# Node stages in quads, edge attributes by the pair, and the second MLP product as four 64x64 quadrants

## The chip, the core and the metric

The kernel runs on one core of a Trainium2 chip. The metric is the device time of one execution in microseconds (us); lower is better. Its engines are TensorE (PE; loading its weights is PEld), VectorE (DVE), ScalarE (ACT), GpSimd (POOL) and the DMA engines; SP issues most of the DMAs.

## The reference

One graph attention layer in fp32 with a residual, for 12,500 nodes of 128 features and 400,000 edges sorted by destination:

```python
h = relu(layernorm(x))
msg_src = h @ w_src + b_src
msg_dst = h @ w_dst
rad = silu(silu(edge_attr_32 @ w1 + b1) @ w2 + b2) @ w3 + b3      # 32 -> 64 -> 64 -> 128
m = (msg_src[src] + msg_dst[dst]) * edge_weight * rad
a, v = per head of 8: (m @ w_sep + b_sep)                          # 16 + 16 columns a head
score = sum(leaky(a) * alpha_dot)
att = softmax of score over the edges of one destination
out = x + segment_sum(v * att, dst) @ w_proj + b_proj
```

## The kernel before

**Node stage.** The nodes are 98 blocks of 128 rows (the last has 84). They are loaded at once and taken in groups of 14 blocks. `stats` (L196 to L201, DVE and ACT) and `norm` (L209, ACT) make the normalised rows of group g + 1, then `products` turns and multiplies group g in quads of four blocks: transposes into PSUM (L220, PE), a copy to hT (L223, DVE), products with w_src and w_dst side by side (L230, PE), the source half copied out by ACT (L237), the destination half by DVE with b_src added (L238). Every group ends with two stores into the tables t_src and t_dst. After the second group `ends_and_cuts` compares the destinations and writes the ends of the sections. A branch on `bad` follows; then `windows` zeroes and loads the block-diagonal weights (w1b, w2b, w3b, b12), computes b_s, and reads the ends back (L606 to L641).

**Loop.** The edges are 400 pairs of two sections of 500. `step(k)` is called for k = -5 to 399 and 14 times more; its statement order is each engine's order, since scheduling is manual. It handles several pairs at once: loads on SP for k + 3; eight indirect gathers on POOL of t_src rows for pair k + 4 (L718, four buffers `gs`, each freed by the transposes of its pair); for pair k the third MLP product (L758), rad on DVE (L761), the transposes of the gathered rows and the destination part into pm (L770, L775), their product with rad, mT (L779); for pair c = k - 12 the value products (L864, L866) and the sums over destinations (L875), whose PSUM tile misc ACT copies to ob (L879) and SP stores; for pair k the attention product (L783, L785, L787); the first MLP product of pair k + 2 (L736, h1 on ACT L739), the second of k + 1 (L744, h2 on ACT L746); the turned attributes of k + 3 (L728 into bank m1, L730). Odd steps end with the scores (L794, also in misc), steps with k mod 8 = 3 turn the softmax (L838, also in misc).

The order of TensorE's work in a step is third product, L770, L775, values of section 0, attention of section 0, values of section 1, first product, second product, attention of section 1, sums, turned attributes, scores. The second product is one matmul of 128x128 weights (two 64x64 blocks on the diagonal, the rest zero) by 500 columns, and its bank m1 is also the one that the turned attributes use. The first and the third product use the two banks of p3. An fp32 matmul shows up as two instructions in the profile.

Attributes come in groups of eight pairs, by eight strided DMAs (L693), two in the first step of a group, one in each of the next six and none in the last.

**Final stage.** After the loop and a last scatter into agg (L1067), the nodes are taken in groups of 14: x + b_out on POOL (L1162), the quotients by the softmax sums on DVE (L1165 to L1168), then in quads the transposes (L1179, PE), qT (L1182, ACT), a correction added to x on DVE (L1185), the product with w_proj (L1186, PE), its sum with x (L1190, DVE), and one store for a group.

Of the kernel before, what the change touches and what calls it, by code (L numbers as in the profile page):

```python
# [30 lines left out]
P = 128  # L31
C = 128
# [21 lines left out]
EP = 8  # L54
# [3 lines left out]
def gnn_kernel(ctx: ExitStack, tc: tile.TileContext, a: dict, out: bass.AP):  # L58
# [18 lines left out]
    agg = dram.tile([N + W, ROW], F32, name="agg")  # L77
    win = dram.tile([NS * W, ROW], F32, name="win")
    base_d = dram.tile([2, NP], I32, name="base_d")
# [15 lines left out]
    x_v = x[0:NF * P, :].rearrange("(p t) c -> p t c", t=NF)  # L95
    ident = const.tile([P, P], F32, name="ident")
# [48 lines left out]
    with tc.tile_pool(name="node", bufs=2) as np_, tc.tile_pool(name="node1", bufs=1) as n1, \  # L145
# [6 lines left out]
        b_nodes = n1.tile([P, C], F32, name="b_nodes")  # L152
        nc.scalar.dma_start(out=b_nodes, in_=a["b_src"].to_broadcast([P, C]))
# [6 lines left out]
        last = n1.tile([1, 2, NP], I32, name="last")  # L160
# [3 lines left out]
        nc.sync.dma_start(out=prev[1:RP, :], in_=dst[RC - 1:E - 1].rearrange("(p c) -> p c", c=RC))  # L164
        with nc.allow_non_contiguous_dma(reason="the sections' ends"):
            for f in range(2):
                nc.sync.dma_start(out=base[:, f, :], in_=dst_h[f:f + 1, :, 0])
                nc.sync.dma_start(out=last[:, f, :], in_=dst_h[f:f + 1, :, SEC - 1])
# [16 lines left out]
        spans = groups[:-1] + [(groups[-1][0], NB)]  # L185
        hs = {}

        def rows(t):
            return P if t < NF else tail

        def stats(g):
            t0, t1 = spans[g]
# [11 lines left out]
        def norm(g):  # L204
            t0, t1 = spans[g]
            hs[g] = np_.tile([P, XG, C], F32, name="h")
            for t in range(t0, t1):
                n = rows(t)
                nc.scalar.activation(hs[g][:n, t - t0, :], x_all[:n, t, :], AF.Relu,  # L209
                                     bias=shift[:n, t:t + 1], scale=rstd[:n, t:t + 1])  # L210

        def products(g):
            t0, t1 = spans[g]
            ms = np_.tile([P, 2, XG, C], F32, name="ms")
            for u0 in range(t0, t1, 4):
                us = range(u0, min(u0 + 4, t1))
                pt = nps.tile([P, 4, P], F32, name="pt")
                for u in us:
                    n = rows(u)
                    nc.tensor.transpose(pt[:, u - u0, :n], hs[g][:n, u - t0, :], ident[:n, :n])  # L220
                hT = np_.tile([P, 4, P], F32, name="hT")
                w = (len(us) - 1) * P + rows(us[-1])
# [58 lines left out]
        for g in range(G):  # L281
# [4 lines left out]
            if g == 1:  # L286
                ends_and_cuts()
# [950 lines left out]
```

## Time and profile before

| | |
|---|---|
| median of 3 runs | 6550.76 us (6549.27 to 6562.26) |
| profiled execution, its own time | 6566.2 us |
| its span | 6564.2 us |
| mean TensorE clock granted | 0.873 |
| busy: PE, DVE, ACT, POOL | 77%, 44%, 27%, 47% |
| first gather, first L770 | 215.9 us, 240.5 us |
| last ob, first data of the final stage | 6393.9 us, 6424.7 us |
| DMA packets | 884,920, of them 527,255 under 512 B |

Busy time is that of the engine's instructions in the profiled execution; the end of a matmul is modelled. A row of the costliest groups gives line, engine, operation, out<-in, shapes and count, then busy us and mean ns of one, then the engine's idle time just before these instructions and what ended most of it. In a timeline row the bracket holds the idle time before the instruction and its releaser. A row of a stretch gives start:end, its length, busy us (and instructions) of PE, PEld, DVE, ACT and POOL, the granted clock as a share of full speed, the DMA engines' busy share and GB/s.

### The profile page before, as it was taken

How to read it: one execution, taken by the hardware profiler on the slowest of the kernel's cores; microseconds unless marked ns; L12 is line 12 of the kernel's file. 1: busy time of each engine (PE TensorE's matmuls, PEld its weight loads, DVE VectorE, ACT ScalarE, POOL GpSimd, SP SyncE). 2: the span in 40 equal slices, each digit the busy share in tenths (PEclk: the TensorE clock that was granted, in tenths of full speed). 3: DMA queues.
4: the chain of work that ended last, by engine and by line, in shares of the span. 5: the costliest groups of instructions: out<-in, count | busy, mean ns of one | idle time of the engine just before them, and what ended most of it. 6: DMA issues, size and time to landing. Idle time of an engine off the chain costs nothing. (4 is left out here: it accounts for less than half of the span.)

```text
span 6564.2 us, 79188 instructions
## 1 busy us (share of the span) xinstructions
PE 5066.2 (77%) x26490; PEld 2665.6 (41%) x26490; DVE 2887.1 (44%) x5210; ACT 1785.1 (27%) x3797; POOL 3111.5 (47%) x3231
## 2 busy tenths in 40 slices
PE   3477878787878878788788787887887878888774
PEld 2234444444444444444444444444444444444453
DVE  4234444444444444444444444444444444444465
ACT  3122222222222222222222222222222222222221
POOL 0455555455554545544455454454554545545402
PEclk7688898898998989988888898898888989888885
DMA  3454444444444444444444444444444444444423
GB/s 124 135 144 119 124 119 115 125 117 121 121 122 118 121 119 119 124 117 115 123 120 121 119 116 121 122 115 120 121 117 122 119 120 121 124 119 118 114 60 123
DMA packets 884920, 783.25 MB, mean 119 GB/s; under 512 B 527255, under 2 KB 773279, under 8 KB 884250
## 3 DMA queue, kind: packets, MB, share of 16 engines
q1 hardware_dynamic: 778482, 560.72, 31.0%
q0 software_dynamic: 102816, 210.37, 13.6%
q10 hardware_dynamic: 3202, 6.99, 0.3%
q8 instruction: 212, 3.47, 0.2%
q14 instruction: 208, 1.70, 0.1%
HBM read 643.82 MB, written 134.27 MB: 119 GB/s over the span
## 5 line engine op out<-in xcount | busy, mean ns | idle before, releaser
L718 POOL DMA_INDIRECT gs<-t_src,idx x3200 | 3067.4, 959 | 3189.3 <-PE pm L770 1756.2
L787 DVE SCALAR_TENSOR_TENSOR al<-pa,sl 128x500 f32<-128x500 f32 x800 | 542.9, 679 | 1570.9 <-ACT sl L785 1022.1
L761 DVE SCALAR_TENSOR_TENSOR rad<-p,c_fc_b,w_b 128x500 f32<-128x500 f32 x800 | 553.6, 734 | 1389.4 <-PE p L758 1102.0
L783 PE MATMUL pa<-mT,c_w_a 128*128 128x500 f32 x1600 | 833.7, 603 | 256.8 <-DVE mT L779 248.1
L785 ACT ACTIVATE sl<-pa,c_b_a 128x500 f32<-128x500 f32 x800 | 541.4, 677 | 1789.4 <-PE pa L783 626.9
L864 PEld LDWEIGHTS V<-c_w_v,mT 128*125 128x125 f32 x6208 | 741.2, 188 | 634.8 <-issue 337.9
L864 PE MATMUL V<-c_w_v,mT 128*125 128x128 f32 x6208 | 891.3, 286 | 23.2 <-issue 1.1
L794 PE MATMUL misc<-al,w_s 128*32 128x500 f32 x1600 | 365.9, 986 | 539.5 <-ACT ob L879 525.3
L779 DVE TENSOR_TENSOR mT<-pm,rad 128x500 f32<-128x500 f32 x800 | 504.3, 672 | 280.1 <-PE pm L775 252.8
L758 PE MATMUL p<-h,w3b 64*128 64x500 f32 x1600 | 625.5, 870 | 0.0
L770 PEld LDWEIGHTS pm<-ident,gs 125*128 125x128 f32 x3200 | 430.1, 169 | 435.9 <-issue 435.9
L866 DVE TENSOR_TENSOR pvx<-V,Pem 125x512 f32<-125x512 f32 x776 | 528.9, 682 | 44.4 <-PE m L744 26.5
L770 PE MATMUL pm<-ident,gs 125*128 125x125 f32 x3200 | 533.6, 321 | 0.0
L875 PEld LDWEIGHTS misc<-pvx,oh 125*64 125x64 f32 x6400 | 365.5, 137 | 322.4 <-issue 279.7
L875 PE MATMUL misc<-pvx,oh 125*64 125x136 f32 x6400 | 473.0, 287 | 28.2 <-DVE pvx L866 27.6
L783 PEld LDWEIGHTS pa<-mT,c_w_a 128*128 128x128 f32 x1600 | 269.5, 191 | 500.6 <-DVE mT L779 287.4
L775 PE MATMUL pm<-ohT,md 64*128 64x500 f32 x1600 | 471.0, 656 | 0.1
L739 ACT ACTIVATE h<-p,b 128x500 f32<-128x500 f32 x400 | 270.5, 676 | 700.9 <-PE pa L783 157.2
L879 ACT COPY ob<-misc 128x136 f32<-128x136 f32 x400 | 108.7, 272 | 1292.5 <-remote 630.5
L744 PE MATMUL m<-h,w2b 128*128 128x500 f32 x800 | 449.6, 644 | 0.0
L728 PE MATMUL m<-ident,e_t 125*128 125x125 f32 x800 | 187.4, 319 | 204.4 <-ACT h L746 169.8
L746 ACT ACTIVATE h<-m,b 128x500 f32<-128x500 f32 x400 | 270.7, 677 | 223.4 <-PE m L744 55.0
(145 smaller groups left out, 3153.1 us busy)
## 6 DMA issues: line engine op xcount, KB each, us to landing
w_b<-in_edge_weight SPq DMA_DIRECT2D x400, 500.0 KB
d_b<-in_dst SPq DMA_DIRECT2D x400, 250.0 KB
gs<-t_src,idx POOLq DMA_INDIRECT x3200
e_t<-in_edge_attr SPq DMA_DIRECT2D x400, 125.0 KB
sc_d<-Sp SPq DMA_DIRECT2D x200, 250.0 KB
win<-ob SPq DMA_DIRECT2D x400, 68.0 KB
agg<-ob SPq DMA_DIRECT2D x800, 33.5 KB
md<-t_dst SPq DMA_DIRECT2D x800, 32.0 KB
```

Of the source, the lines that this page charges most:

```text
L718: nc.gpsimd.indirect_dma_start(out=gs[:, j, :], out_offset=None, in_=t_src[:, :], in_offset=bass.IndirectOffsetOnAxis(ap=idx[:, t:t + 1], ...
L758: nc.tensor.matmul(p3[:, f, 0:SEC], w3b[s, :], h2s[k][s, :], start=True, stop=True)
L761: nc.vector.scalar_tensor_tensor(rads[f], p3[:, f, 0:SEC], b3, w_g[k][:, f * SEC:(f + 1) * SEC], op0=ALU.add, op1=ALU.mult)
L770: nc.tensor.matmul(pm[f][:, t * T:(t + 1) * T], gs[:T, f * TS + t, :], ident[:T, :T], start=(t == 0), stop=False, is_transpose=True, skip_ ...
L775: nc.tensor.matmul(pm[f], md[k][s, :], ohT[k][s, :], start=False, stop=True, skip_group_check=True)
L779: nc.vector.tensor_mul(mTs[k][:, f * SEC:(f + 1) * SEC], pm[f], rads[f])
L783: nc.tensor.matmul(pa, w_a, mTs[k][:, f * SEC:(f + 1) * SEC], start=True, stop=True)
L785: nc.scalar.activation(sl, pa, AF.Silu, bias=b_a, scale=1.0)
L787: nc.vector.scalar_tensor_tensor(al, pa, 0.25, sl, op0=ALU.mult, op1=ALU.add)
L864: nc.tensor.matmul(V[:, t, :], mTs[c][:, o:o + T], w_v, start=True, stop=True)
L866: nc.vector.tensor_mul(pvx[c][:, f, :, 0:C].rearrange("p t (h k) -> p t h k", h=H), V.rearrange("p t (h k) -> p t h k", h=H), Pem[c // MP] ...
L875: nc.tensor.matmul(acc[f * W:(f + 1) * W, :], ohs[c][:, f * TS + t, :], pvx[c][:, f, t, :], start=(t == 0), stop=(t == TS - 1), skip_group ...
```

## The change

- The node stage runs by quads: statistics two quads at a time, norms two quads ahead, transposes one quad ahead. Both halves of a product leave PSUM in one copy, on ACT but for one in eight on DVE, and each quad is stored by two DMAs. b_src is no longer added here but where mT is made, for each of 400 x 2 sections (one scalar_tensor_tensor instead of a multiply).
- The MLP weights, b_s, v_out and what is read back of the ends are prepared within the node stage; `fits` and `cuts` take the place of `ends_and_cuts`.
- One DMA loads the attributes of one pair, six steps ahead, with four buffers.
- The second product consists of four matmuls with 64x64 weights by 250 columns, at the four quadrants of the array, into two banks of p3; the activations for h1 and h2 read and write through rearranged views. The first product moves ahead of the values of section 1, the second behind the attention of section 1, directly ahead of the sums. Bank m1 is left to the turned attributes.
- x + b_out is made in the loop: from step 40 on, every eighth step loads a quad of x, two steps later DVE adds b_out and SP stores it to xb.
- The final stage reads xb, takes groups of 12 for the quotients (a group ahead), turns a quad ahead, writes the result over x and stores every quad.

```diff
-        b_nodes = n1.tile([P, C], F32, name="b_nodes")
-        nc.scalar.dma_start(out=b_nodes, in_=a["b_src"].to_broadcast([P, C]))
...
+            s = slice(f * FC, (f + 1) * FC)
+            for q in range(2):
+                nc.sync.dma_start(out=w2b[s, q * FC:(q + 1) * FC], in_=a["fc_w2"])
+            nc.sync.dma_start(out=w3b[s, :], in_=a["fc_w3"])
...
+        b_n = load("b_n", [C, 1], a["b_src"].rearrange("o c -> c o"))
...
-        def norm(g):
-            t0, t1 = spans[g]
-            hs[g] = np_.tile([P, XG, C], F32, name="h")
+        def norm(i):
+            t0, t1 = quads[i]
+            hs[i] = np_.tile([P, 4, C], F32, name="h", bufs=3)
             for t in range(t0, t1):
                 n = rows(t)
-                nc.scalar.activation(hs[g][:n, t - t0, :], x_all[:n, t, :], AF.Relu,
+                nc.scalar.activation(hs[i][:n, t - t0, :], x_all[:n, t, :], AF.Relu,
                                      bias=shift[:n, t:t + 1], scale=rstd[:n, t:t + 1])
-        def products(g):
-            t0, t1 = spans[g]
-            ms = np_.tile([P, 2, XG, C], F32, name="ms")
...
+        def turn(i):
...
+        def products(i):
+            t0, t1 = quads[i]
+            hT = hTs.pop(i)
+            ms = np_.tile([P, 2, 4, C], F32, name="ms", bufs=4)
+            for v0 in range(t0, t1, 2):
+                vs = range(v0, min(v0 + 2, t1))
+                pm = nps.tile([P, 2, 2, C], F32, name="pm", bufs=4)
+                for t in vs:
+                    n = rows(t)
+                    nc.tensor.matmul(pm[:n, t - v0], hT[:, t - t0, :n], w_nodes, start=True, stop=True)
+                for n, u0, u1 in blocks(v0, vs[-1] + 1):
+                    o, q = ms[:n, :, u0 - t0:u1 - t0, :].rearrange("p k j c -> p j k c"), pm[:n, u0 - v0:u1 - v0]
+                    if v0 % 16 == 2:
+                        nc.vector.tensor_copy(o, q)
...
+                        nc.scalar.copy(o, q)
...
+            nc.sync.dma_start(out=eb.rearrange("p s i -> p (s i)"),
+                              in_=ends_d[0:1, 1:2 * NS + 1].to_broadcast([P, 2 * NS]))
...
+        def cuts():
...
+            nc.vector.tensor_sub(far, eb[:, :, 1], eb[:, :, 0])
+            for f in range(2):
+                q = slice(f * W, (f + 1) * W)
+                nc.vector.tensor_scalar(tgt[q, :], eb[q, f::2, 0], part[q, :], float(f * W),
+                                        op0=ALU.add, op1=ALU.subtract)
...
+        stats(0, 4)
         norm(0)
-        for g in range(G):
-            if g + 1 < G:
-                stats(g + 1)
-                norm(g + 1)
-            products(g)
-            if g == 1:
-                ends_and_cuts()
-        w_score = const.tile([C, C], F32, name="w_score")
-        nc.vector.tensor_scalar(w_score, heads, dot, 0.8, op0=ALU.mult, op1=ALU.mult)
+        stats(4, G)
+        norm(1)
+        turn(0)
+        for i in range(Q):
+            if i % 2 == 0 and 4 * i + G < NB:
+                stats(4 * i + G, min(4 * i + 2 * G, NB))
+            if i + 2 < Q:
+                norm(i + 2)
+            if i + 1 < Q:
+                turn(i + 1)
+            products(i)
+            if i == 12:
+                fits()
+        cuts()
...
-            def load_e(g, i):
-                if i == 0:
-                    e_g[g] = lp.tile([T, EP * 8, RAD], F32, name="e_t")
-                f, t = divmod(i, TS)
-                o = t % 2 * 4 + t // 2 * 2 + f
-                nc.sync.dma_start(out=e_g[g][:, o::8, :],
-                                  in_=ea_t[:, g * 8 * EP + i:(g + 1) * 8 * EP:8, :])
+            def load_e(k):
+                e_g[k] = lp.tile([T, 8, RAD], F32, name="e_t", bufs=4)
...
             def mlp1(k):
                 p1 = pp.tile([P, 2, BANK], F32, name="p3")
                 for q in range(2):
                     s = slice(q * 2 * RAD, (q + 1) * 2 * RAD)
                     nc.tensor.matmul(p1[:, q, 0:2 * T], w1b[s, :], eTs[k][s, :],
                                      start=True, stop=True)
                 h1s[k] = sp.tile([P, SEC], F32, name="h1")
-                nc.scalar.activation(h1s[k].rearrange("p (q e) -> p q e", q=2), p1[:, :, 0:2 * T],
+                nc.scalar.activation(h1s[k].rearrange("x (f q p) -> x q f p", f=2, q=2),
+                                     p1[:, :, 0:2 * T].rearrange("x q (f p) -> x q f p", f=2),
                                      AF.Silu, bias=b12[:, 0:1], scale=1.0)
             def mlp2(k):
-                p2 = pp.tile([P, SEC], F32, name="m1")
-                nc.tensor.matmul(p2, w2b, h1s.pop(k), start=True, stop=True)
+                p2 = pp.tile([P, 2, BANK], F32, name="p3")
+                h1 = h1s.pop(k)
+                for h in range(2):
+                    s = slice(h * FC, (h + 1) * FC)
+                    for f in range(2):
+                        o = slice(f * FC, (f + 1) * FC)
+                        nc.tensor.matmul(p2[o, h, 0:2 * T], w2b[s, o], h1[s, f * 2 * T:(f + 1) * 2 * T],
+                                         start=True, stop=True)
                 h2s[k] = sp.tile([P, SEC], F32, name="h2")
-                nc.scalar.activation(h2s[k], p2, AF.Silu, bias=b12[:, 1:2], scale=1.0)
+                nc.scalar.activation(h2s[k].rearrange("x (q h p) -> x h q p", q=2, h=2),
+                                     p2[:, :, 0:2 * T].rearrange("x h (q p) -> x h q p", q=2),
+                                     AF.Silu, bias=b12[:, 1:2], scale=1.0)
...
-                    nc.vector.tensor_mul(mTs[k][:, f * SEC:(f + 1) * SEC], pm[f], rads[f])
+                    s = slice(f * SEC, (f + 1) * SEC)
+                    nc.vector.scalar_tensor_tensor(mTs[k][:, s], pm[f], b_n, rad[:, s], op0=ALU.add, op1=ALU.mult)
...
+            def load_x(i):
+                xs[i] = lp.tile([P, 4, C], F32, name="xs")
+                for n, t0, t1 in blocks(*quads[i]):
+                    o = quads[i][0]
+                    nc.sync.dma_start(out=xs[i][:n, t0 - o:t1 - o, :],
+                                      in_=x_v[:, t0:t1, :] if n == P else x[NF * P:N, :].unsqueeze(1))
+            def add_x(i):
+                t = xs.pop(i)
+                for n, t0, t1 in blocks(*quads[i]):
+                    u = t[:n, t0 - quads[i][0]:t1 - quads[i][0], :]
+                    nc.vector.tensor_tensor(u, u, b_out[:n].unsqueeze(1).to_broadcast([n, t1 - t0, C]), op=ALU.add)
+                    nc.sync.dma_start(out=xb_v[:, t0:t1, :] if n == P else xb[NF * P:N, :].unsqueeze(1), in_=u)
...
-            for i in range(8):
-                load_e(0, i)
+            for k in range(2):
+                load_e(k)
...
-                g, r = divmod(k + 3, EP)
-                if k >= -3 and r < EP - 1 and has((g + 1) * EP):
-                    for i in ((0, 1) if r == 0 else (r + 1,)):
-                        load_e(g + 1, i)
+                if has(k + 6) and k >= -4:
+                    load_e(k + 6)
...
+                i, q = divmod(k - 40, MP)
+                if 0 <= i < Q and q == 5:
+                    load_x(i)
+                if 0 <= i < Q and q == 7:
+                    add_x(i)
...
                     alphas(k, 0)
+                if has(k + 2):
+                    mlp1(k + 2)
                 if has(c):
                     values(c, 1)
-                if has(k + 2):
-                    mlp1(k + 2)
+                if has(k):
+                    alphas(k, 1)
                 if has(k + 1):
                     mlp2(k + 1)
                     one_hot_T(k + 1)
-                if has(k):
-                    alphas(k, 1)
                 if has(c):
                     sums(c)
                 m, r = divmod(k, MP)
...
-        bvb = f1.tile([C, P], F32, name="bvb")
-        nc.vector.tensor_copy(bvb, b_v.to_broadcast([C, P]))
-        pv = fps.tile([P, C], F32, name="pv", bufs=1)
-        nc.tensor.matmul(pv, bvb, w_proj, start=True, stop=True)
-        v_out = f1.tile([P, C], F32, name="v_out")
-        nc.vector.tensor_copy(v_out, pv)
...
+            nc.scalar.dma_start(out=x_all[:, t0:t1, :], in_=xb_v[:, t0:t1, :])
...
-                nc.gpsimd.tensor_tensor(x_all[:n, t0 + a0:t0 + a1, :], x_all[:n, t0 + a0:t0 + a1, :],
-                                        b_out[:n].unsqueeze(1).to_broadcast([n, a1 - a0, C]), op=ALU.add)
...
+            t0, t1 = quads[i]
+            qT = qTs.pop(i)
+            py = fps.tile([P, 4, C], F32, name="py")
+            for t in range(t0, t1):
+                n = rows(t)
+                nc.tensor.matmul(py[:n, t - t0, :], qT[:, t - t0, :n], w_proj, start=True, stop=True)
+            for t in range(t0, t1):
+                n, u = rows(t), t % XQ
+                xt = x_all[:n, t, :]
+                nc.vector.scalar_tensor_tensor(xt, v_out[:n], has[t0 // XQ][:n, u:u + 1], xt,
+                                               op0=ALU.mult, op1=ALU.add)
+            for n, u0, u1 in blocks(t0, t1):
+                y = x_all[:n, u0:u1, :]
+                nc.vector.tensor_add(y, py[:n, u0 - t0:u1 - t0, :], y)
+                nc.sync.dma_start(out=out_v[:, u0:u1, :] if n == P else out[NF * P:N, :].unsqueeze(1), in_=y)
+        NG = len(starts)
+        for i in range(3):
             load_g(i)
-            if i >= 3:
-                finish(i - 3)
-        for i in range(len(groups) - 3, len(groups)):
+        quotients(0)
+        turn(0)
+        for i in range(Q):
+            if i % 3 == 0 and i // 3 + 3 < NG:
+                load_g(i // 3 + 3)
+            if i % 3 == 1 and i // 3 + 1 < NG:
+                quotients(i // 3 + 1)
+            if i + 1 < Q:
+                turn(i + 1)
             finish(i)
```

## Prediction

> **What bounds the kernel now.** I read the page's busy times and costliest groups, then the timeline of two steps in mid-loop, last the busy times by stage. The page invites the wrong answer:
>
> ```profile
> PE 5066.2 (77%) x26490; PEld 2665.6 (41%) x26490; DVE 2887.1 (44%) x5210; ACT 1785.1 (27%) x3797; POOL 3111.5 (47%) x3231
> ...
> L718 POOL DMA_INDIRECT gs<-t_src,idx x3200 | 3067.4, 959 | 3189.3 <-PE pm L770 1756.2
> ...
> L879 ACT COPY ob<-misc 128x136 f32<-128x136 f32 x400 | 108.7, 272 | 1292.5 <-remote 630.5
> ```
>
> TensorE is busiest, but see the idle columns: L879, the copy of a step's sums out of PSUM, has 1292.5 us of idle ACT before it (3.2 us a step), and the gathers have 1756.2 us in which POOL waits for L770. The timeline shows why (start, duration, engine, line; first an odd step, then the even one after it):
>
> ```profile
> 3003.91 0.27 ACT L879 COPY ob<-misc 128x136 f32<-128x136 f32 x1 [3.11 <-remote]
> ...
> 3008.03 1.93 PE L770 MATMUL pm<-ident,gs 125*128 125x125 f32 x8
> ...
> 3010.23 0.94 POOL L718 DMA_INDIRECT gs<-t_src,idx  x1 [8.16 <-PE pm L770]
> ```
>
> ```profile
> 3014.64 1.10 PE L744 MATMUL m<-h,w2b 128*128 128x500 f32 x2
> ...
> 3016.51 1.15 PE L875 MATMUL misc<-pvx,oh 125*64 125x136 f32 x16
> ...
> 3018.96 0.94 POOL L718 DMA_INDIRECT gs<-t_src,idx  x1 [0.30 <-issue]
> ...
> 3021.63 0.27 ACT L879 COPY ob<-misc 128x136 f32<-128x136 f32 x1 [4.34 <-PE pm L775]
> ```
>
> Gathers start 1.25 us apart: the first of this step at 3010.23, the eighth at 3018.96. The sums (L875) end at 3017.66, yet ob starts at 3021.63, 2.67 us after the eighth gather's start; the next gather follows at 3022.24, although L770 was over at 3020.06. Over 360 steps of the trace ob starts 2.55 to 3.14 us (5th to 95th percentile) after the eighth gather's start, so I take the gathers, not the sums, to release it; what connects the two the trace does not say. A step is then 8.74 us (first to eighth gather) + 2.73 (median) + the time from ob to the next first gather: 0.61 after even steps, median 6.32 after odd ones, where scores (L794, 1.90), third product (L758, 2.04) and transposes (1.93) follow ob in turn. That makes 12.1 and 17.8 us; the trace has 12.18 and 18.24, mean 15.21. TensorE's work from L770 to the sums lies under some 4 us of slack.
>
> The ends have other limits (stretch, length, busy PE, PEld, DVE, ACT, POOL, then clock):
>
> ```profile
> 5.70:193.50 187.80, 83.69 (x296) 62.87 (x296) 90.46 (x298) 58.93 (x156) 0.00 (x0) 0.78 0.30 111
> 193.50:215.90 22.40, 1.05 (x10) 0.73 (x10) 3.81 (x17) 0.00 (x0) 0.04 (x1) 0.51 0.47 150
> 6424.70:6564.20 139.50, 70.53 (x294) 58.05 (x294) 90.20 (x159) 16.14 (x29) 29.72 (x8) 0.54 0.32 125
> ```
>
> In the node stage (first) and the final stage (last) no engine reaches two thirds: they take turns. The costliest groups of the final stage:
>
> ```profile
> L1185 DVE SCALAR_TENSOR_TENSOR x_fin<-v_out,has,x_fin 128x128 f32<-128x128 f32 x98 | 49.4, 562 | 0.0
> L1186 PE MATMUL py<-c_w_proj,qT 128*128 128x128 f32 x196 | 48.9, 422 | 24.6 <-ACT qT L1182 18.2 <-DVE y L1190 6.4
> ...
> L1179 PE MATMUL pt<-ident,q 128*128 128x128 f32 x98 | 25.9, 410 | 44.3 <-DVE q L1168 40.6 <-DVE r L1165 3.6
> ```
>
> L1186 and L1179 wait 24.6 and 44.3 us for other engines: that is what lookahead can take away.
>
> **The sum** is made against the profiled run (6566.2 us; span 6564.2 and 2 around it). It lies 15.4 us above the median 6550.76; differences are carried over to the median.
>
> *Node stage.* PE does L230 (68.7) and L220 (19.6) = 88.3 us. ACT after: 98 norms at a pace of 0.385 = 38, 42 two-block copies at 0.68 (the 128x500 ACT rows) = 29: 67. DVE: statistics 98 x 0.395 = 39, hT 17, seven copies 5, scales 5, the order test 7: 73. With norms two quads and transposes one quad ahead, PE bounds it: 10 lead-in + 88 + 12 for joints, order test and last quad = 110 at the end instead of 193.5: **-83**. (All gaps gone: -93; half left: -45.)
>
> *Setup.* Between 193.5 and the first gather (215.9) lie the branch (5), twelve weight loads, three loads of ends (0.6 us each on SP's queue), index loads and index making. The weights go under the node stage; the DVE work of the cuts (sm 3.5 + 1.0, some 3 of small pieces) comes out behind it. 6 + 5 + 1.5 + 3.5 + 2.4 = 18.4 against 22.4: **-4**. Eight attribute loads on SP in front of the first step (2 us each, 209.9 to 225.3) become two; the first gathers wait for none of them, so I count nothing (up to -10).
>
> *Attributes by the pair.* As many packets; two issues back to back in every eighth step (the second took 3.84 us) become one a step. No path: **0**.
>
> *Second product.* Two instructions take 0.94 us start to start. Its nearest row after is L736, whose row tiles overlap (four instructions of 250 columns in 0.63 us to the next start); the quadrants issue eight. Were both directions to overlap as rows do, 0.63: -0.31 a step, -124 in all. One after another: 8 x 0.235 (half of 0.47, one 500-column instruction) = 1.88, +0.94 a step, +376. I take 0.63, nearest the row. The Trainium skill's "TensorEngine Tiling (Array Packing)", Key Properties, speaks against it: changing the tiling mode drains TensorE, and here 128x128, 64x64 and 128x64 follow one another. The trace already changes mode between L783 (128x128) and L875 (128x64): 0.93 us start to start against 0.94 from L744 to L783, without a change. The row prices a drain at about 0; the rule, at worst one L783 instruction (0.6 us), at +240. Either way the cover is the 4 us between sums and ob: I count **0**; with the cover gone the bounds are -124 and +616.
>
> *Order and banks.* p2 leaves bank m1, for which e_T waited on h2 204.4 us in all (L728), 1.24 us of it in steps with k mod 8 = 0, which last 13.0 us against 11.9 of other even ones. I take half of 1.1 x 50: **-25** (0 to -55). p2 now shares p3 with both other products; the first product comes a V group (1.1) and a pa (1.0) ahead, and h1 takes 0.68, so PE seldom waits.
>
> *mT with the bias.* 672 ns becomes a row of the kind of L787 or L761 (679, 734): 800 x 0.01 to 0.06, under the slack: **0** (at most +50).
>
> *x + b_out in the loop.* 25 loads and stores of 256 KB and 25 adds on DVE (about 0.7). Each store waits for DVE on SP's queue, with the next step's store of ob and its loads behind it; those run three to six steps ahead: **0** (at most 25 x 1).
>
> *Final stage.* POOL's adds go; while they ran four L1185 took 16 us instead of 1.13. From g's landing (6424.7): quotients 3 + transposes 1.1 + qT 0.7, then PE bounds, 48.9 + 25.9 = 75 plus 5 of joints; DVE has 98 x 0.283 + L1190's 17.6 + quotients 24 = 69. Then y 1 and the last store 5: 6515.5 instead of 6564.2: **-48** (-25 to -60).
>
> Total -83 - 4 - 25 - 48 = -160: 6566.2 - 160 = 6406 profiled, 6391 by the median.
>
> **Rivals.**
> *The second product on the path:* if TensorE's order and not the gathers sets the step, the 0.31 us come back: 6391 - 124 = 6267. For it: PE 77% busy, no idle before L744. Against: the fixed 2.73 us.
> *The hold catches h2 (slower):* the second product now stands directly ahead of the sums, whose completion is seen only with the release. If its own is, too, then in even steps third product and transposes come after the release: +2.16 us (the odd 0.61 becomes 2.77, its 95th percentile), and in odd steps h2's 0.7 comes ahead of ob. In all steps 200 x 2.86 = +572: 6960. It outweighs the ends from (83 + 4 + 25 + 48)/2.86 = 56 pairs of steps on. Against: pa of the second section stands in that place now, and its sl was late by over 1 us in 32 of 769 cases.
> *Lookahead half effective:* clock and joints cost more: ends -70, loop 0: 6481.
>
> **How the numbers follow.** Forecast (6340 to 6450): 0.50. On the path: 0.12. Half effective: 0.14. Hold: 0.20, most of it for only part of the steps, so anywhere from 6560 to 6960. The remaining 0.04: loop and ends cancel within 0.2% (13 us, about what a measurement of this kernel can tell from no change). The range, 6260 to 6620, leaves out the lower edge of the second case and the hold in over a third of the steps. Faster 0.76, same 0.04, slower 0.20.
>
> **What would show it.** Right: first L770 near 150 instead of 240.5; final stage some 91 us from g's landing; PE's time for the second product a third lower with the same mean step; ob still 2.7 us after the eighth gather. Wrong: an even step over 12.5 us with the h2 copy starting together with ob (hold); a mean step under 15 us with ob directly after the sums (on the path); quadrants starting 0.2 us or more apart (no overlap).

## The result and the profile after

| | before | after |
|---|---|---|
| median of 4 runs each, same chip | 6552.52 us | 6955.28 us (6931.72 to 6967.0) |
| ratio, 95% interval | 1 | 1.0608 [1.0576, 1.0639]: slower |
| span of the profiled execution | 6564.2 us | 6929.9 us |
| mean TensorE clock granted | 0.873 | 0.836 |
| first gather, first L770 (after: L790) | 215.9, 240.5 us | 162.8, 172.0 us |
| step, mean of pairs 12 to 380 | 15.20 us | 16.49 us |
| even steps, odd steps (from third product to third product) | 12.17, 18.23 us | 14.58, 18.39 us |
| last ob to the span's end | 170.3 us | 107.7 us |

The forecast was 6391 us (6260 to 6620). The measured time lies outside that range and beside that of the rival called the hold, 6960. The 366 us between the spans come from these stretches: up to the transposes of pair 12, -64; pairs 12 to 380, +473; from there to the last ob, +19; after it, -63. The loop lost almost four times what the two ends gained (127).

The page of after, busy line and costliest groups (L777 is the third product, L763 makes h2, L815 the scores):

```profile
PE 5155.1 (74%) x28892; PEld 2711.9 (39%) x28892; DVE 2958.5 (43%) x5205; ACT 1762.2 (25%) x3795; POOL 3136.9 (45%) x3223
...
L726 POOL DMA_INDIRECT gs<-t_src,idx x3200 | 3122.4, 976 | 3564.4 <-PE pm L790 2515.7
...
L777 PE MATMUL p<-h,w3b 64*128 64x500 f32 x1600 | 734.7, 1012 | 602.6 <-ACT h L763 596.8
...
L815 PE MATMUL misc<-al,w_s 128*32 128x500 f32 x1600 | 373.1, 1019 | 555.7 <-ACT ob L900 536.8
...
L763 ACT ACTIVATE h<-p,b 128x500 f32<-128x500 f32 x400 | 271.5, 679 | 1214.2 <-remote 974.2
```

The same two rows of before, the third product and h2:

```profile
L758 PE MATMUL p<-h,w3b 64*128 64x500 f32 x1600 | 625.5, 870 | 0.0
...
L746 ACT ACTIVATE h<-m,b 128x500 f32<-128x500 f32 x400 | 270.7, 677 | 223.4 <-PE m L744 55.0 <-PE pa L783 53.5 <-issue 52.5
```

The new wait is that of L777: TensorE stands idle for 596.8 us until h2 is there, where the third product of before (L758) waited 0.0. L763, which makes h2, has 1214.2 us of idle ACT ahead of it (223.4 before). POOL's gathers wait 2515.7 us for the transposes, 760 more than before. The wait of the scores for ob (536.8) was there before (525.3).

An even step of after on the timeline (start, duration, engine, line):

```profile
3025.04 0.65 PE L760 MATMUL p<-h,w2b 64*64 64x250 f32 x8
...
3025.62 1.15 PE L896 MATMUL misc<-pvx,oh 125*64 125x136 f32 x16
...
3028.38 0.68 ACT L763 ACTIVATE h<-p,b 128x500 f32<-128x500 f32 x1 [2.20 <-PE m L736]
...
3029.01 0.95 POOL L726 DMA_INDIRECT gs<-t_src,idx  x1 [0.30 <-issue]
...
3029.12 1.69 PE L777 MATMUL p<-h,w3b 64*128 64x500 f32 x4 [1.99 <-ACT h L763]
...
3030.74 1.93 PE L790 MATMUL pm<-ident,gs 125*128 125x125 f32 x8
3031.31 0.27 ACT L900 COPY ob<-misc 128x136 f32<-128x136 f32 x1 [2.25 <-PE pm L790]
...
3032.94 0.94 POOL L726 DMA_INDIRECT gs<-t_src,idx  x1 [2.99 <-PE pm L790]
```

The quadrants end at 3025.69, and ACT is idle from 3026.18 on, yet h2 starts at 3028.38: 2.7 us late. Third product and transposes shift behind it, so that the transposes last until 3032.67 and the next gather follows at 3032.94, 1.63 us after ob, where before it was 0.61. Over the loop h2 starts 4.30 us (even steps) and 4.23 (odd) after the end of the quadrants, before 1.31 and 0.61. A part of this is ACT's own work: another of its instructions can still run when the product ends. Counted from the moment at which the product has ended and ACT is free, h2 starts 3.12 us (even) and 3.08 (odd) late, before 0.42 and 0.30.

How much h2 may be late could be read in before: there the third product started 0.93 us (mean) after the end of h2 in even steps and 7.33 in odd ones. In even steps h2 now comes 2.99 us later (4.30 - 1.31); less that slack, 2.06 us should be lost, and in odd steps nothing. The cycle from gather to gather, means over the loop in us (its steps begin elsewhere than those of the table above):

| | 1st to 8th gather | to ob | ob to next gather |
|---|---|---|---|
| even, before / after | 8.77 / 9.01 | 2.80 / 2.80 | 0.90 / 2.93 |
| odd, before / after | 8.78 / 8.86 | 2.77 / 3.01 | 6.42 / 6.34 |

Of 2.51 us for two steps, 2.03 lie in one cell, from ob to the next gather after an even step, close to the 2.06.

### The profile page after: what moved, and what is told of

It reads as the page before. It is cut to its first block, busy times and chain, and to the rows that moved or that the text cites. A ratio compares the mean times of both kernels' runs of the same rounds, so it can differ in the third digit from the quotient of the medians.

```text
span 6929.9 us, 84197 instructions
## 1 busy us (share of the span) xinstructions
PE 5155.1 (74%) x28892; PEld 2711.9 (39%) x28892; DVE 2958.5 (43%) x5205; ACT 1762.2 (25%) x3795; POOL 3136.9 (45%) x3223
## 4 chain that ended last, share of the span: by engine, by line
PE 63%; another core or an unknown queue 18%; ACT 9%; issue 5%; DVE 3%; DMA 1%; SPq 1%; POOL 0%; ACTq 0%; POOLq 0%; DVEq 0%
PE V L885 10%; PE p L777 10%; PE pa L804 9%; PE pm L790 9%; PE pm L795 7%; PE misc L815 5%; PE p L760 3%; ACT sl L806 3%; PE p L745 3%; PE misc L896 2%; ACT h L763 2%; PE m L736 2%; ACT ob L900 1%; PE misc L859 1%
## 5 line engine op out<-in xcount | busy, mean ns | idle before, releaser
L726 POOL DMA_INDIRECT gs<-t_src,idx x3200 | 3122.4, 976 | 3564.4 <-PE pm L790 2515.7
L777 PE MATMUL p<-h,w3b 64*128 64x500 f32 x1600 | 734.7, 1012 | 602.6 <-ACT h L763 596.8
L815 PE MATMUL misc<-al,w_s 128*32 128x500 f32 x1600 | 373.1, 1019 | 555.7 <-ACT ob L900 536.8
L800 DVE SCALAR_TENSOR_TENSOR mT<-pm,c_b_n,rad 128x500 f32<-128x500 f32 x800 | 553.5, 733 | 497.3 <-PE pm L795 438.3
L790 PEld LDWEIGHTS pm<-ident,gs 125*128 125x128 f32 x3200 | 511.8, 193 | 524.6 <-issue 524.4
L896 PE MATMUL misc<-pvx,oh 125*64 125x136 f32 x6400 | 560.5, 290 | 168.4 <-DVE pvx L887 125.4
L790 PE MATMUL pm<-ident,gs 125*128 125x125 f32 x3200 | 632.8, 363 | 1.6 <-issue 1.6
L763 ACT ACTIVATE h<-p,b 128x500 f32<-128x500 f32 x400 | 271.5, 679 | 1214.2 <-remote 974.2
L777 PEld LDWEIGHTS p<-h,w3b 64*128 64x128 f32 x1600 | 184.6, 282 | 934.2 <-ACT h L763 642.9
L795 PE MATMUL pm<-ohT,md 64*128 64x500 f32 x1600 | 518.9, 729 | 0.0
L745 PE MATMUL p<-eT,w1b 64*128 64x250 f32 x1600 | 280.1, 427 | 1.0 <-ACT eT L738 1.0
L815 PEld LDWEIGHTS misc<-al,w_s 128*32 128x32 f32 x1600 | 40.0, 137 | 608.9 <-ACT ob L900 571.2
L748 ACT ACTIVATE h<-p,b 128x500 f32<-128x500 f32 x400 | 271.1, 678 | 22.5 <-remote 10.5
```

The costliest lines, as they stand in the source:

```text
L726: nc.gpsimd.indirect_dma_start(out=gs[:, j, :], out_offset=None, in_=t_src[:, :], in_offset=bass.IndirectOffsetOnAxis(ap=idx[:, t:t + 1], ...
L777: nc.tensor.matmul(p3[:, f, 0:SEC], w3b[s, :], h2s[k][s, :], start=True, stop=True)
L790: nc.tensor.matmul(pm[f][:, t * T:(t + 1) * T], gs[:T, f * TS + t, :], ident[:T, :T], start=(t == 0), stop=False, is_transpose=True, skip_ ...
L795: nc.tensor.matmul(pm[f], md[k][s, :], ohT[k][s, :], start=False, stop=True, skip_group_check=True)
L800: nc.vector.scalar_tensor_tensor(mTs[k][:, s], pm[f], b_n, rad[:, s], op0=ALU.add, op1=ALU.mult)
L815: nc.tensor.matmul(ps[32 * j:32 * j + 32, :], w_s, als.pop(2 * k - 2 + j), start=True, stop=True)
```

## The experiments

Ratios are against the kernel before on the same chip; before itself took 6531 to 6624 us on the chips used. "Step" is the mean of pairs 12 to 380 in the profile, "lag" the mean time from the end of the second product to the start of h2, even/odd steps. For the kernel before they are 15.20 and 1.31/0.61, on the chip of the result, where its median was 6552.52 us. On a chip on which before takes 6624 us its step would be some 15.4 (an estimate, in proportion), so steps from different chips are compared only roughly; the ratios decide. "pa" is the attention product of a section.

**Is it the place or the form of the product?** Two kernels exchange one of the two. In after, the quadrants go one pa ahead of the sums:

```diff
+                if has(k + 1):
+                    mlp2(k + 1)
+                    one_hot_T(k + 1)
                 if has(k):
                     alphas(k, 1)
-                if has(k + 1):
-                    mlp2(k + 1)
-                    one_hot_T(k + 1)
```

> The changed kernel with one thing moved: the second product (still four quadrants in two p3 banks) and its one-hot stand ahead of the attention product of section 1 instead of behind it, so a pa (about 1.0 us of TensorE) lies between it and the sums. Theory A (hold by place: what TensorE finishes directly ahead of or with the sums is seen only about 2.7 us after the eighth gather's start, and h2 with it): h2 starts within 1 us of the quadrants' end in most steps, the mean step (pairs 12 to 380) falls from 16.49 to about 15.2 us, the time to 6430 to 6500 us. Theory B (the quadrants themselves, by drains of the array or by sharing p3 with the other two products): the step stays at 16.3 us or more, the time at 6870 to 6960 us.

Measured: 6748.54 us, 1.0305 [1.0268, 1.0343]; step 16.01, lag 4.20/4.07. Neither theory came true as stated: h2 stays late, against A, but the step falls below B's 16.3. In before, the one matmul goes to after's place and bank, with the first product in after's place, too:

```diff
-                p2 = pp.tile([P, SEC], F32, name="m1")
+                p2 = pp.tile([P, 2, BANK], F32, name="p3")[:, 0, 0:SEC]
...
```

> The kernel before, its second product still one 128x128 by 500 matmul, but in the order of the changed kernel (first product ahead of the values of section 1, second directly ahead of the sums) and in the first p3 bank instead of m1. Theory A: even steps last 2 us or more longer, the time is 6950 to 7080 us. Theory B: within 1% of the kernel before, 6490 to 6620 us.

Measured: 6562.43 us, 1.0018 [1.0006, 1.0029]; step 15.23, lag 1.35/0.92. This is theory B. The place and the bank alone cost next to nothing; the quadrants are late in either place, though the place is worth 3% once they are. The reason that the prediction gave for the hold, standing directly ahead of the sums, falls.

**Do the gathers make it late?** Two kernels change them. Five buffers instead of four in before:

```diff
-                gs = lp.tile([P, 8, C], F32, name="gs", bufs=4)
+                gs = lp.tile([P, 8, C], F32, name="gs", bufs=5)
```

> The kernel before with five gather buffers instead of four: a pair's first gather then waits for the transposes of the step before, not of its own step. If the release of TensorE's completions hangs on the eighth gather (what the prediction's chain says), the eighth gather and ob come several us earlier, and the mean step falls from 15.2 to 12.5 to 14 us: 5500 to 6100 us. If ob is late for a reason of its own (its stores, the DMA queues), the step stays at 15 us or more: 6450 to 6560 us.

Measured: 6547.09 us, 1.0004 [0.9991, 1.0018]; step 15.16. The step is what was expected if ob is late for a reason of its own. But a fifth buffer only changes which pair a batch belongs to: as in before, a batch starts 11.5 us ahead of an ob, and that ob comes some 2.8 us after the batch's eighth gather. So this run settles nothing on the cause. The second kernel gathers for the first four pairs only and uses their rows again for all later ones, so its rows of the sources are not the reference's:

```diff
+                if k >= 4:
+                    gs = gath[k - 4]
-                for j in range(8):
+                for j in range(8 if k < 4 else 0):
```

> The kernel before with the gathers of the first four pairs only; the later pairs reuse these four buffers, so their messages are those of other edges. If the gathers hold TensorE's completions, ob starts within 0.2 us of the sums' end in nearly all steps and the mean step is 9.7 to 11.5 us (the last steps of the kernel before, which have no gathers, take some 10): 4400 to 5100 us in all. If not, ob stays 3 to 4 us behind the sums and the mean step is over 12 us.

Measured: 4916.03 us in one run; step 10.99, granted clock 0.963. Its timeline (here L746 is the second product, L748 h2, L877 the sums, L881 ob):

```profile
2807.59 1.10 PE L746 MATMUL m<-h,w2b 128*128 128x500 f32 x2
...
2808.74 0.68 ACT L748 ACTIVATE h<-m,b 128x500 f32<-128x500 f32 x1 [0.35 <-PE m L746]
...
2809.47 1.15 PE L877 MATMUL misc<-pvx,oh 125*64 125x136 f32 x16
...
2810.66 0.27 ACT L881 COPY ob<-misc 128x136 f32<-128x136 f32 x1 [0.41 <-PE misc L877]
```

h2 follows its product after 0.05 us (2807.59 + 1.10 = 2808.69), ob the sums after 0.04, and so in all steps, where ob was 4.0 us late with gathers. Both latenesses belong to the gathers. Their instructions on POOL and their DMA transfers went together here, so which of the two it is this run can't tell.

**Which property of the quadrants?** They differ from one matmul in column tiles, row tiles and number. First two column tiles, then two halves of the columns at the full array, both in before's place; then the quadrants themselves in before, one pa ahead of the sums, with the bank, the rearranged activations and the earlier first product that belong to them:

```diff
...
+                    o = slice(f * FC, (f + 1) * FC)
+                    nc.tensor.matmul(p2[o, :], w2b[:, o], h1, start=True, stop=True)
```

> The kernel before, its second product as two matmuls on column tiles (128x64 weights by 500 columns each, same bank m1, same place, same result). Theory C: completions of matmuls on column tiles (the sums and the quadrants are such) are seen late while gathers run: h2 starts 3 us or more after the product's end in most steps, the mean step is 15.8 us or more, the time 6700 to 6950 us. Theory D (it is the number of instructions in a short time): as its neighbour with two halves, which issues as many.

```diff
...
+                    o = slice(f * 2 * T, (f + 1) * 2 * T)
+                    nc.tensor.matmul(p2[:, o], w2b, h1[:, o], start=True, stop=True)
```

> The kernel before, its second product as two matmuls with the full 128x128 weights by 250 columns (as many matmuls and weight loads as with two column tiles, none on part of the array). Theory C: as before, 6500 to 6600 us, h2 within 1 us of the end in most steps. Theory D: h2 late by 3 us or more, time over 6700 us.

```diff
...
+                        nc.tensor.matmul(p2[o, h, 0:2 * T], w2b[s, o], h1[s, f * 2 * T:(f + 1) * 2 * T],
+                                         start=True, stop=True)
...
```

> The kernel before with the second product as four quadrants in p3 with the rearranged activations (attributes still loaded in groups, in the order that these need), placed one pa ahead of the sums as in the first experiment; the ends and all else as before. If the quadrants alone make the loss of the loop, the mean step is within 0.2 us of the first experiment's 16.01: 6810 to 6930 us. If another part of the change makes it, the step is 15.0 to 15.5: 6480 to 6640 us.

And the other way round, the whole change but with one matmul for the second product, in before's order and bank, and with before's grouped attribute loads (the expectations call this kernel the fifth experiment; C and D are the theories just stated):

```diff
-                        nc.tensor.matmul(p2[o, h, 0:2 * T], w2b[s, o], h1[s, f * 2 * T:(f + 1) * 2 * T],
-                                         start=True, stop=True)
...
+                nc.tensor.matmul(p2, w2b, h1s.pop(k), start=True, stop=True)
...
```

> The changed kernel with the loop's second product, its order and the attribute loads as before (one 128x128 by 500 matmul into m1, groups of eight pairs); kept are both ends, x + b_out in the loop, the weights' place and the bias in mT. Theories C and D below both put the whole loss into the quadrants: mean step 15.1 to 15.4 us, h2 within 1 us of the product's end in most steps, time 6380 to 6470 us. If the loss comes from what is kept (mT, the loads of x, SP's queue), the step stays over 15.8 us: over 6600 us.

All four ran on the chip on which before takes 6624 us. The last column counts from when ACT is free:

| second product | ratio [95%] | step | lag | from free ACT |
|---|---|---|---|---|
| two column tiles (2 matmuls) | 1.0172 [1.0132, 1.0213] | 15.78 | 3.16/2.79 | 1.52/1.81 |
| two halves (2 matmuls) | 1.0215 [1.0162, 1.0268] | 15.66 | 2.71/2.73 | 1.35/1.81 |
| quadrants in before (4 matmuls) | 1.0732 [1.0692, 1.0771] | 16.64 | 5.12/4.20 | 5.13/4.20 |
| one matmul, rest of after | 0.9831 [0.9792, 0.9869] | 15.39 | 1.85/1.65 | 0.54/0.85 |

Halves without any tiling are about as late as column tiles: from one matmul to two it is the number that counts, not the tiling. For four this is argued, not shown: no run has four matmuls over the whole array, or quadrants outside p3 without other changes. Added to before, the quadrants cost 7.3%, more than the 6810 to 6930 us expected (7105.05); without them the rest of the change gains 1.7% (6524.57 us; the expected 6380 to 6470 were missed on this slower chip, and h2 is later than the expected 1 us). So the quadrants are the loss, whichever way it is tried. Two other products, each as halves in before, ask whether every added matmul counts: first both attention products (two matmuls more a step), then both third products:

```diff
...
+                    o = slice(h * 2 * T, (h + 1) * 2 * T)
+                    nc.tensor.matmul(pa[:, o], w_a, mTs[k][:, f * SEC + h * 2 * T:f * SEC + (h + 1) * 2 * T],
+                                     start=True, stop=True)
```

> The kernel before, each attention product (500 columns) as two of 250: two more matmuls a step, in the stretch in which gathers run, none on part of the array. Theory D (what TensorE finishes is seen the later, the more instructions it has issued while gathers run): as with the second product in two halves, +0.3 to 0.45 us a step and matmul, ratio 1.03 to 1.06. If only the second product is so sensitive, ratio under 1.01.

```diff
...
+                        o = slice(h * 2 * T, (h + 1) * 2 * T)
+                        nc.tensor.matmul(p3[:, f, o], w3b[s, :], h2s[k][s, o], start=True, stop=True)
```

> The kernel before, the third product (two row tiles by 500 columns) as four by 250: two more matmuls a step, but at its start, before the step's gathers; in odd steps no gather is in flight then. Theory D: a much smaller loss than with the attention product, ratio under 1.02. If every matmul that is added costs alike, 1.03 to 1.06.

Measured: 1.0106 [1.0072, 1.014], step 15.35, lag 1.99/1.08; and 1.0006 [0.9988, 1.0024], step 15.19, lag 1.31/0.73. The added attention matmuls, which stand on both sides of the second product, cost less than was expected; the third product's cost nothing. So not every matmul costs time. The lateness grew there, too: the reader of the attention product of section 1 starts 1.22/1.44 us late, from free ACT, where it was 0.37/0.40. What is lost depends on the slack of the reader. Half of each sum left out (two of four tiles) asks what ob follows:

```diff
-                for t in range(TS):
+                for t in range(2):
...
```

> The kernel before, each section's sums over two of its four tiles only (half of the edges are left out of the sums): four matmuls a step fewer, directly ahead of ob. Gate: if ob is released by the eighth gather, it still starts 2.7 us after that gather's start, though the sums end some 0.5 us earlier, and the time stays within 1%. Backlog: if TensorE's completions queue up by number, ob starts 1 us or more sooner after the eighth gather, and the time falls by 2% or more.

Measured: 6478.5 us in one run, 0.8% under before; step 15.00. ob still comes 2.65 us (median) after the eighth gather's start, in before 2.73: the gathers set it, the length of the sums hardly.

**Is the lag the whole cost?** Then a product with a step of slack may be late for nothing. First product, second product and turned attributes were moved one step ahead, for one matmul, two halves and the quadrants (these in after, with banks m1 and V and two activations of 250 columns):

```diff
...
+                if has(k + 3):
+                    mlp1(k + 3)
...
+                if has(k + 4):
+                    e_T(k + 4)
...
+                    mlp2(k + 2)
...
```

> The fifth experiment's kernel (ends of the change, one second product) with attributes, first and second product made one step earlier, so that h2 has a whole step before the third product asks for it. If late h2 alone makes the loop's differences, the mean step is at or a little under the kernel before's 15.20: 14.9 to 15.3 us, ratio 0.965 to 0.983.

> The same with the second product as two matmuls of 250 columns. In the kernel before these cost 0.46 us a step, with h2 seen 1.8 us later than with one. If that lateness is the whole cost, the mean step is within 0.15 us of the run with one product a step ahead. If instructions cost by themselves, it is 0.35 us or more above it.

> The changed kernel with attributes, first and second product one step earlier and the four quadrants in banks m1 and V instead of p3, so that neither the third product nor its bank waits for h2 (two activations of 250 instead of one of 500). If late h2 is what the quadrants cost, the mean step falls from 16.49 to 15.0 to 15.4 us: ratio 0.965 to 0.985. If the quadrants slow TensorE itself, it stays over 15.9 us: ratio over 1.0.

Measured: steps of 15.38, 15.41 and 15.32; ratios 0.9922 [0.9896, 0.9948], 0.9941 [0.9921, 0.9961], 0.9967 [0.9947, 0.9987]. With slack one, two and four matmuls give the same time within 0.5%, where without it four cost 7.8% of before more than one (1.0608 against 0.9831): the lag is the cost of the quadrants, and their shorter time on TensorE gains nothing. For the halves only the step moved; with the quadrants the banks did, too. The slack is not free: the ratios of 0.965 to 0.983 and 0.985 expected for the first and the third kernel were missed, and one matmul takes 0.9922 with slack, 0.9831 without. Why was not tried.

**Can the scores be freed of ob?** The sums share misc with the scores, which therefore wait for the late ob. Two kernels, made from the one with one product, move the sums to m1; in both the second product goes to p3 and the first ahead of the values of section 1, which cost nothing in before (1.0018). In the first (the ninth experiment of the expectations) the turned attributes have the other half of the same tile:

```diff
-                acc = pp.tile([P, ROW], F32, name="misc")
+                both[0] = pp.tile([P, BANK], F32, name="m1")
+                acc = both[0][:, BANK // 2:BANK // 2 + ROW]
...
```

> A version of our own: the fifth experiment's kernel (both ends of the change, one 128x128 by 500 second product, groups of attributes) with this product in the first p3 bank, one pa ahead of the sums, and with the sums in the free half of the m1 bank, so that scores and the turned softmax, which use misc, need not wait for the copy ob. By the prediction's chain the odd steps then go on like the even ones: about 12.5 to 13.5 us a step, 5450 to 5900 us in all (ratio 0.83 to 0.89). If the wait only moves to the next use of a late completion (the scores' own, al or h2), the step stays at 14.5 us or more: ratio over 0.95.

Measured: 1.0987 [1.095, 1.1024], step 17.10. The turned attributes, which share the tile, now waited for ob in 383 of 400 steps, 4.2 us (median); even steps rose to 15.96. The expectation missed this new wait. In the second the sums have m1 alone, and what was in m1 goes to p3 and misc; the turned attributes and the turned softmax stand ahead of the sums:

```diff
-                pe = pp.tile([P, 2, T], F32, name="m1")
+                pe = pp.tile([P, 2, T], F32, name="misc")
...
-                acc = pp.tile([P, ROW], F32, name="misc")
+                acc = pp.tile([P, ROW], F32, name="m1")
...
```

> The ninth experiment mended: there the turned attributes shared a tile with the sums and waited for ob in every step. Here the sums have bank m1 alone, the second product p3, and the turned attributes and the turned softmax stand ahead of the sums in misc, so that nothing of TensorE's queue waits for ob. By the chain the odd steps lose their wait: mean step 12.5 to 14 us, ratio 0.82 to 0.91. If another late completion takes its place (h2, al or the turned attributes), 14.5 us or more, ratio over 0.94.

Measured: 5744.82 us, **0.8792 [0.8766, 0.8819]**, step 13.43, clock 0.930: the fastest kernel here, ahead of before and after. Its page (L731 gathers, L810 scores):

```profile
PE 4732.4 (82%) x26492; PEld 2629.9 (46%) x26492; DVE 2930.2 (51%) x5206; ACT 1796.8 (31%) x3795; POOL 3119.8 (54%) x3223
...
L731 POOL DMA_INDIRECT gs<-t_src,idx x3200 | 3105.3, 970 | 2402.1 <-PE pm L785 962.8
...
L810 PE MATMUL misc<-al,w_s 128*32 128x500 f32 x1600 | 266.4, 683 | 181.8 <-issue 104.6
```

The kernel with one product, from which it differs by these moves, has:

```profile
L731 POOL DMA_INDIRECT gs<-t_src,idx x3200 | 3063.6, 957 | 3217.4 <-PE pm L785 1827.2 <-issue 842.4 <-PE pm L790 321.2
...
L810 PE MATMUL misc<-al,w_s 128*32 128x500 f32 x1600 | 376.7, 987 | 463.5 <-ACT ob L895 444.6 <-ACT Pem L856 15.8 <-DVE al L803 2.8
```

There the scores had 463.5 us of idle time, 444.6 of it for ob, and the gathers waited 1827.2 us for the transposes; now these are 181.8, with ob not named, and 962.8. The time from ob to the next gather in odd steps was 6.32 us (median) there and is 2.48. ob itself still comes 2.8 us after the eighth gather.

## Why the prediction was wrong, point by point

*What bounds the loop*: right. ob follows the eighth gather's start by 2.70 us (even) and 3.20 (odd, median) after the change, 2.65 with half the sums, and the lateness vanishes without gathers.

*Second product: "Either way the cover is the 4 us between sums and ob: I count 0"*: this step failed. The time on TensorE was forecast well: the quadrants take 0.58 us to the next start where 0.63 was taken (0.94 before). But the 4 us between sums and ob cover TensorE's work, not the wait of its readers. h2 is late like ob, and it heads the chain of third product, transposes and gathers, which had 0.93 us of slack behind h2 in even steps, not 4. h2 came 2.99 us later there, L777 waits 596.8 us, and the loop grew by 473. The +473 lies within the bounds given for the cover gone (-124 to +616), but by luck: those were bounds of TensorE's time, which fell.

The drain, by which the Trainium skill's "TensorEngine Tiling (Array Packing)", Key Properties, spoke against the change, hardly shows. From the start of the attention product ahead to the start of the quadrants it takes 1.00 us, to one matmul at the same place (the second run above) 0.91: 0.09 us is what a drain ahead of them could be, and from there to the sums 0.58 against 0.93. The prediction chose the measured row over the rule, and rightly, but on a question that was not the one that mattered.

*The hold as a rival, chance 0.20*: near in size, right in part of its mechanism, wrong in its reason. From ob to the next gather in even steps it has +2.16, measured +2.03; in odd steps +0.7, measured +0.16. Its sign, h2 starting together with ob, holds for some steps only: h2 starts less than 0.8 us ahead of ob in 80 of 184 even and 118 of 184 odd steps, in the others earlier (2.93 us in the step shown). The place ahead of the sums is not the reason, as the first two runs show. That its 6960 lies beside the measured 6955 is in part luck: the loop lost less than its 572 us, and the ends gained less than forecast. It was weighed by pa, late in 32 of 769 cases; pa is one matmul, the quadrants are four. Counted alike, from when ACT is free, h2 of before was late by over 1 us in 46 of 400 steps, so no row of before gave the lag of four matmuls away. What it did show was how little slack h2 had.

*Node stage, -83*: it ended at 147.8 instead of the forecast 110. Stretches as in the prediction's table (node stage, setup, final stage):

```profile
6.00:147.80 141.80, 77.66 (x298) 55.91 (x298) 70.66 (x264) 66.22 (x157) 0.00 (x0) 0.80 0.44 155
147.80:162.80 15.00, 1.55 (x13) 1.08 (x14) 5.37 (x17) 0.00 (x0) 0.00 (x0) 0.64 0.38 118
6840.00:6929.90 89.90, 44.34 (x294) 42.15 (x294) 65.79 (x164) 15.56 (x26) 2.90 (x4) 0.77 0.59 220
```

The missing 37.8 us are one stall. The waits of the node stage (engine, what it waits for; us, times, longest), and below them SP's queue on the timeline:

```profile
DVE ms L259 <- DMA t_dst<-ms: 37.8, 1, 37.8
ACT ms L261 <- DMA t_dst<-ms: 36.6, 1, 36.6
```

```profile
32.55 13.64 SPq L177 DMA_DIRECT2D ends<-in_dst  x1
...
46.32 18.70 SPq L188 DMA_DIRECT2D w1b<-in_fc_w  x2
...
68.23 1.04 SPq L188 DMA_DIRECT2D w1b<-in_fc_w  x2
...
72.46 0.52 SPq L266 DMA_DIRECT2D t_src<-ms  x1
...
75.69 0.58 ACT L261 COPY ms<-pm 128x512 f32<-128x512 f32 x1 [36.60 <-DMA t_dst<-ms]
```

The four buffers of ms were full, and their stores, the first of which is issued at 72.46, stood on SP's queue behind the loads of the ends (13.64 us), of w1b (18.70 for two) and of the other weights. The size of w1b is not the reason for the 18.70, since two more loads of it take 1.04; what held the first two is not shown. In before loads of the ends held the queue until 60.3, too, but there a group of 14 blocks was stored at once and later. New are the stores by the quad, which need the queue early, and the weights ahead of them. The prediction wrote "the weights go under the node stage" and did not price the queue. 147.8 - 37.8 = 110, the forecast end, but not term by term: PE was busy for 77.7 us where 88 were summed. That the stall is worth this much was read, not tried.

*Setup, -4*: 15.0 us from the stage's end to the first gather, against 18.4; -7.4 against the 22.4 of before.

*Final stage, -48*: -60.3, from the first data (6850.7) to the end 79.2 us instead of 139.5; the sum had some 91. It took 422 ns for each L1186 from before; with the granted clock at 0.77 instead of 0.54 the same instruction (now L1235) took 317, 31.9 us in all instead of 48.9, and not PE but DVE, busy 65.8 of these 79.2 us (69 in the sum), is the bound.

*Order and banks, -25*: the wait of the turned attributes on h2 is gone from the trace, but even steps as a whole are longer, so that its worth cannot be separated.

*mT, x + b_out and the rest, 0*: holds as far as can be told. The kernel with one product has all of these and takes 99.6 us less than before on its chip (6524.57 against 6624.15). In the profiles its ends gain some 113 us on before's (50 up to the transposes of pair 12, 63 after the last ob; the profiles are from two chips), which leaves an estimated 13 us for the loop, within the bounds given (50 and 25).

**Open.** The end of a matmul is modelled, so the records cannot tell whether quadrants and sums end late or are only seen late. What links the gathers to it was not found; POOL's instructions and the DMA transfers of the gathers were not tried apart. Nor is it clear why quadrants in before (16.64) take 0.63 us a step more than in after at the same place (16.01); some 0.2 of it is the slower chip (6624 against 6545 us for before).

## What to carry to other kernels

A product that is shorter on its engine is worth nothing while another wait sets the step, and can cost much when its reader's lag grows: price an edit by when its reader starts, and look in the trace of before at how much later that reader may start before something waits for it; here that was 0.93 us, not the 4 us of a neighbour. Where a result is seen late for a reason that can't be removed, give it a step of slack or take its tile away from what stands behind it; here the slack took back the 6% that the change had cost, and the tile was worth 10.6% (0.8792 against 0.9831). A load moved under another stage is hidden only if no store that is needed soon stands behind it on its queue.

## What the runs showed of the hardware

- While the indirect gathers run, the readers of TensorE's results start late: ob 4.0 us after the sums in before, h2 (from free ACT, means of the kernels without the step of slack) by 0.3 to 1.4 us after one matmul, 1.4 to 1.8 after two and 3.1 to 5.1 after the four quadrants. Without gathers it is 0.04 to 0.05 us. What links them stays open.
- Without gathers the granted clock was 0.963, in before 0.873, in after 0.836 and in the fastest kernel 0.930.
- A load of the sections' ends, 6.2 KB, held SP's queue for 13.64 us, and two loads of a small weight behind it 18.70, where two more of the same weight took 1.04.
- Changing between tile shapes cost at most some 0.1 us: from the attention product's start to the quadrants' 1.00 us, to one matmul at the same place 0.91. The quadrants themselves take 0.58 us to the next start, one matmul 0.93.
